# Two layers of graph network and expert mixture: the first expert pages on bytes of their own, and the other pages' transposes moved from three pairs ahead of their products to five

## The chip, the cores and the metric

The kernel runs on one core of one Trainium2 chip. The metric is the device time of one execution in microseconds; it is given as the median of a few runs. The five engines of the core are TensorE (PE, matrix products and transposes; its weight loads are listed as PEld), VectorE (DVE), ScalarE (ACT), GpSimd (POOL) and SyncE (SP). Each engine runs its own instructions in order; semaphores order them against one another. "SPq" and "ACTq" are the DMA queues that SyncE and ScalarE fill; the indirect DMAs of this kernel are issued by GpSimd.

## The reference

The input x has 8,192 tokens (128 graphs of 64 nodes) of 256 numbers, in 32-bit floats. Two layers follow each other, and each has a graph part and an expert part:

```python
x = x + _L0_gnn_ref(_layernorm(x), adj, ...)
x = x + _L0_ffn_ref(_layernorm(x), ...)
x = x + _L1_gnn_ref(_layernorm(x), adj, ...)
x = x + _L1_ffn_ref(_layernorm(x), ...)
```

The change lies in the expert part of layer 0. Each token picks six of 64 experts, and each expert is one 256 x 256 matrix:

```python
def _L0_ffn_ref(x, gate_w, lattice_weights, out_w, out_b, ln_g, ln_b):
    logits = jnp.einsum('bsd,ed->bse', x, gate_w)
    top_logits, indices = jax.lax.top_k(logits, 6)
    scores = jax.nn.softmax(top_logits, axis=-1)
    W_sel = lattice_weights[indices]
    xW = jnp.einsum('bsd,bskde->bske', x, W_sel)
    lattice_out = jnp.einsum('bske,bsk->bse', xW, scores)
    proj = jnp.einsum('bsd,ed->bse', lattice_out, out_w) + out_b
    ...
```

So 8,192 x 6 = 49,152 products of a token's row with its expert's matrix are needed, and their order is free. The graph part of layer 0 (`_L0_gnn_ref`) multiplies each graph's tokens by its adjacency matrix and passes them through a two-layer network of width 1,024; layer 1 is built alike, with eight experts of two matrices each and two experts a token.

## The kernel before

**The stages.** The kernel has four stages, one after the other.

1. Layer 0's graph part and its routing, in 32 blocks of 256 tokens (the long list of functions that ends at line 791). At its end `place` (L745) calls `send` (L310) for each block: 12 indirect DMAs of GpSimd (L314), one for each half of the block and each of the six choices, write every token's normalized row into a table in DRAM (`r0x`), at the place kept for it among its expert's rows. A table row has W = 258 numbers: the 256 values, the number of the answer's row it belongs to, and the weight of the choice. The rows lie in SBUF in the tile `xs` (three buffers).
2. Layer 0's expert pages (lines 800 to 860). The table is read back in pages of 128 rows that all belong to one expert, so that one page needs one matrix.
3. Layer 1's graph part and routing, in 32 blocks again.
4. Layer 1's expert pages, of 256 rows.

**The early pages.** After block 20 the kernel looks (`look`, L151) which of the first twelve experts (EARLY = 12) already have a full page of 128 rows. Such a page gets no more rows, so it can be read while later blocks are still sent. It is the first page of each of these experts: twelve early pages, in six pairs, numbered -6 to -1. All other pages wait for the page table, which VectorE works out after the last block (`page_table`, L338, 810.4 to 829.9 us in the profile). There are 412 of these, in 206 pairs, and a further few behind a branch (L857), for routings that need them.

**One pair of pages** goes through four steps:

- `fetch` (L808): SyncE loads the two pages (129 KB each) from the table into the tile `px`. It has `bufs=22`: 22 pairs may be in SBUF at once. The load of pair j is asked for 12 pairs ahead of its product. `fetch_first` (L456) is the load of an early page, and doesn't wait for rows that are still on their way; `fetch` of the Router (L460) is that of any other. `load_first` and `load` read the page's row numbers into SyncE's registers, four pages at a time.
- `flip` (L822): TensorE transposes the pair, four blocks of 128 x 128, into PSUM (`pt`, L828), and ScalarE copies the result to SBUF (`pxT`, `bufs=5`, L830).
- `apply` (L832): TensorE multiplies (`py`, eight matmuls, L846), with the matrix taken from the tile `lat`, which holds all 64 experts' matrices. For the early pages the expert's number is fixed; for the others TensorE reads it from the page table. VectorE then scales each row by the choice's weight, from PSUM back into the tile `px` (L848). In the same function `fill_end` (L425) has ScalarE's queue write zeros behind one expert's last row (L193), for the pages that are not full.
- `reply` (L319), also called in `apply`: GpSimd writes the page by an indirect DMA to the rows of the answer (`r0y`, L321), one DMA a page. `px` comes free when this has landed.

**What sets the order.** On TensorE, VectorE and ScalarE the order of the instructions is that in which the Python code issues them (`manual_schedule`). `staggered(n, stages, first)` (L466) does the issuing: in step s it calls each stage's function for pair s - lag. With the list at L852 a step s issues the loads of pair s + 12, the product of pair s, and then the transposes of pair s + 2 if that pair is below 4, or of pair s + 3 if it is 4 or above. Between pairs 3 and 4 two transposes follow one another. On SyncE and GpSimd a scheduler sets the order, by what is ready.

**Where tiles lie.** A tile pool (`tc.tile_pool`) is a stretch of SBUF or PSUM that is given back at the end of its `with` block; the next pool takes the same bytes, and the first use of a new tile waits for the last use of the old tiles that lay there. With `reuse_waits="tile"` these waits go by old tile, not by the whole pool: whoever takes bytes of a tile waits for all uses of that tile. Pools grow from one end of SBUF, those with `side="right"` from the other end. The stage-2 pool `wx0` of the kernel before (px and pxT) is taken as soon as stage 1's pools are given back, and lies on their bytes, among them those of the last blocks' `xs`.

**The expert matrices.** The tile `lat` is as large as all 64 matrices, and parts of it hold other things in stage 1. Seven pieces of four experts are therefore loaded after the last block (L797).

Of the kernel before, what the change touches and what calls it, by code (L numbers as in the profile page):

```python
# [9 lines left out]
F32 = mybir.dt.float32  # L10
# [3 lines left out]
ENG = mybir.EngineType  # L14
MAGIC = 12582912.0
AF = mybir.ActivationFunctionType
ALU = mybir.AluOpType
AX = mybir.AxisListType
PSUM = bass.MemoryType.PSUM
P = 128  # L20
# [445 lines left out]
def staggered(n, stages, first=0):  # L466

    for s in range(first + min(lag for lag, _ in stages), n + max(lag for lag, _ in stages)):
        for lag, f in stages:
            if first <= s - lag < n:  # L470
                f(s - lag)
# [3 lines left out]
def two_layer_gnn_moe_kernel(ctx: ExitStack, tc: tile.TileContext, a: dict, out: bass.AP):  # L475
    nc = tc.nc
    x_in, adjT = a["x"], a["adjT"]
    N, D = x_in.shape
# [3 lines left out]
    KD = D // P  # L482
    T = 2
    C = T * P
    NB = N // C
    E0 = a["L0_ffn_lattice_weights"].shape[0]
# [3 lines left out]
    E1, F1, _ = a["L1_ffn_W2"].shape  # L490
    EARLY = 12
# [9 lines left out]
    ident = const.tile([P, P], F32, name="ident")  # L501
# [57 lines left out]
    r0 = Router(tc, const, small, dram, N, D, E0, K0, T, P, 14 * P, 4, "r0", 3)  # L559
    W = r0.W  # L560
# [3 lines left out]
    lat = lat_pool.__enter__().tile([P, E0, KD, D], F32, name="lat")  # L564
# [18 lines left out]
    with tc.tile_pool(name="c0", bufs=1) as c0, \  # L583
# [28 lines left out]
        late = {}  # L612
# [182 lines left out]
        for i in (0, 5, 2, 3, 1, 6, 4):  # L795
            e = E0 - EB * (i + 1)
            nc.sync.dma_start(out=lat[:, e:e + EB], in_=lat_w[:, e:e + EB])  # L797


    with tc.tile_pool(name="wx0", bufs=3, reuse_waits="tile") as wx, \  # L800
            tc.tile_pool(name="pt1", bufs=4, space=PSUM, reuse_waits="tile") as pt_pool, \
            tc.tile_pool(name="py1", bufs=4, space=PSUM, reuse_waits="tile") as py_pool:
        npair = (r0.pages + 1) // 2
        first = -EARLY // 2
        pairs = {j: dict() for j in range(first, npair)}
        regs = {}

        def fetch(j):  # L808
            Q = pairs[j]
            Q["px"] = px = wx.tile([P, 2, W], F32, name="px", bufs=22)  # L810
            for q in range(2):
                i = 2 * j + q
                if i < 0:
                    if i % 4 == 0:
                        regs["row"] = r0.load_first(i + EARLY, ENG.SP)
                    r0.fetch_first(regs["row"][i % 4], px[:, q:q + 1, :])
                elif i < r0.pages:
                    if i % 4 == 0:
                        regs["row"] = r0.load(0, i, ENG.SP)
                    r0.fetch(i, regs["row"][i % 4], px[:, q:q + 1, :])  # L820

        def flip(j):  # L822
            Q = pairs[j]
            pt = pt_pool.tile([P, KD, C], F32, name="pt")
            n = min(2, r0.pages - 2 * j)
            for q in range(n):
                for k in range(KD):
                    nc.tensor.transpose(pt[:, k, ts(q, P)], Q["px"][:, q, ts(k, P)], ident)  # L828
            Q["xT"] = xT = wx.tile([P, KD, C], F32, name="pxT", bufs=5)
            nc.scalar.copy(xT[:, :, :n * P], pt[:, :, :n * P])  # L830

        def apply(j):  # L832
            Q = pairs[j]
            if 0 <= j < E0:
                r0.fill_end(j)
            if j >= 0 and j % 2 == 0:
                regs["e"] = r0.load(1, 2 * j, ENG.PE)
            py = py_pool.tile([P, 2, D], F32, name="py")
            px, xT = Q["px"], Q["xT"]
            n = min(2, r0.pages - 2 * j)  # L840
            for q in range(n):
                i = 2 * j + q
                for k in range(KD):
                    w = lat[:, i + EARLY, k, :] if i < 0 else \
                        lat[:, ds(regs["e"][i % 4], 1), k, :].rearrange("p o d -> p (o d)")
                    nc.tensor.matmul(py[:, q, :], lhsT=xT[:, k, ts(q, P)], rhs=w, start=(k == 0), stop=(k == KD - 1))  # L846
            for q in range(n):
                nc.vector.tensor_scalar(px[:, q, :D], py[:, q, :], px[:, q, D + 1:D + 2], None, op0=ALU.mult)  # L848
                r0.reply(2 * j + q, px[:, q, :], px[:, q, :D])


        stages = ((-12, fetch), (0, apply),  # L852
                  (-2, lambda j: flip(j) if j < 4 else None), (-3, lambda j: flip(j) if j >= 4 else None))
        likely = (r0.likely_pages - EARLY + 3) // 4 * 2
        staggered(likely, stages, first)
        wait = const.tile([1, 4], F32, name="wait")
        with tc.If(r0.needed(2 * likely)):  # L857
            staggered(npair, stages, likely)

            nc.sync.dma_start(out=wait, in_=r0.answer[0:1, 0:4])  # L860
# [7 lines left out]
    wx = ctx.enter_context(tc.tile_pool(name="wx1", bufs=2, side="right", reuse_waits="tile"))  # L868
# [209 lines left out]
    with tc.tile_pool(name="pt4", bufs=2, space=PSUM, reuse_waits="tile") as pt_pool, \  # L1078
# [4 lines left out]
        regs = {}  # L1083

        likely = r1.likely_pages - FIRST
# [64 lines left out]
        stages = (-2, fetch1), (0, flip1), (1, down), (0, up)  # L1150
# [35 lines left out]
```

## Time and profile before

| What | us |
|---|---|
| Time, median of 3 runs (lowest to highest) | 2091.24 (2089.26 to 2092.26) |
| Profiled execution, first to last instruction | 2457.9 |
| Stage 1 in the profile, about | 0 to 800 |
| Last blocks' routing, page table, last sends | 800 to 845 |
| Layer 0's expert pages | 845 to 1508 |
| Layer 1's graph part | 1509 to 1940 |
| Layer 1's expert pages | 1940 to 2458 |

The profile is one execution under the hardware profiler, which takes longer than the timed ones do; mean granted TensorE clock 0.925. The table below cuts it into stretches. Its columns are the stretch in us and its length, then for each engine the busy time (us) and, in brackets, the number of instructions; then the granted TensorE clock as a share of full speed, the busy share of the DMA engines, and GB/s.

| stretch | length | PE | PEld | DVE | ACT | POOL | PEclk | DMA | GB/s |
|---|---|---|---|---|---|---|---|---|---|
| 800 to 845 | 45 | 10.27 (43) | 8.20 (42) | 27.14 (93) | 2.05 (5) | 25.06 (25) | 0.50 | 0.37 | 114 |
| 845 to 1508 | 663 | 526.06 (2557) | 441.49 (2556) | 178.05 (422) | 117.80 (211) | 410.10 (423) | 0.92 | 0.60 | 178 |
| 1940 to 2458 | 518 | 505.84 (2476) | 445.12 (2474) | 118.92 (368) | 179.56 (414) | 216.90 (141) | 0.99 | 0.68 | 158 |

Read it by row: in the second stretch VectorE and ScalarE are busy for 27% and 18% of the time, GpSimd for 62%, TensorE for 79%; in the third TensorE is busy for 98%. In the first, TensorE has work for 10 of 45 us.

### The profile page before, as it was taken

To read this page: it belongs to the slowest core of one execution; us is meant where nothing else is said; L and a number is where in the kernel's file an instruction comes from. 1 tells how busy PE (TensorE), PEld (TensorE's weight loads), DVE (VectorE), ACT (ScalarE), POOL (GpSimd) and SP (SyncE) were. 2 spreads that over 40 slices of the span, in tenths; PEclk is the share of its full clock that TensorE was granted. 3 is DMA by queue.
4 is the path that set the end of the run, shared out by engine and by line. 5 is a ranking of instruction groups with operands and counts; after the bars stand their busy time and mean duration, and the time that the engine had idled before them with its cause. 6 is when DMAs were issued, how large, how long until landed. Compare 5 with 4: busy or idle time off the path is not lost.

```text
span 2457.9 us, 37031 instructions
## 1 busy us (share of the span) xinstructions
PE 2052.3 (83%) x10564; PEld 1757.6 (72%) x10564; DVE 1190.9 (48%) x3989; ACT 1011.3 (41%) x2037; POOL 1153.4 (47%) x1142
## 2 busy tenths in 40 slices
PE   7887888787875478778777877988898899999998
PEld 6776767676764367666666766877777688888887
DVE  5676767667665522222222223777777522222221
ACT  5666656656654011111111112555555433333332
POOL 0345544554545556666666663233333434444444
PEclk9999889999987689899898998999999899999999
DMA  3223433333325578765555535887675477677775
GB/s 108 89 95 115 128 115 120 127 129 108 111 90 196 162 214 235 213 188 174 171 173 172 158 90 206 279 282 237 228 234 163 111 177 170 156 167 162 161 168 111
DMA packets 284093, 398.96 MB, mean 162 GB/s; under 512 B 56536, under 2 KB 237928, under 8 KB 283888
## 3 DMA queue, kind: packets, MB, share of 16 engines
q1 hardware_dynamic: 204032, 247.67, 34.6%
q0 software_dynamic: 64800, 136.14, 18.7%
q10 hardware_dynamic: 15056, 12.69, 1.6%
q8 instruction: 95, 1.56, 0.3%
q14 instruction: 110, 0.90, 0.1%
HBM read 223.89 MB, written 177.69 MB: 163 GB/s over the span
## 4 chain that ended last, share of the span: by engine, by line
PE 50%; another core or an unknown queue 12%; ACT 8%; DVE 8%; issue 8%; DMA 2%; SPq 2%; POOL 1%; ACTq 0%; DVEq 0%; POOLq 0%
PE py L846 10%; PE ph L1122 9%; PE py L1142 9%; PE ps L913 3%; PE pt L828 3%; PE po L924 3%; PE pz L985 3%; PE pc L996 2%; ACT lat L666 2%; ACT pxT L830 2%; PE ph L663 2%; PE ps L76 1%; SPq L460 1%; ACT xs L715 1%
## 5 line engine op out<-in xcount | busy, mean ns | idle before, releaser
L314 POOL DMA_INDIRECT r0x<-xs,r0row x384 | 388.1, 1011 | 439.8 <-issue 327.9
L846 PE MATMUL py<-lat,pxT 128*128 (+1 forms) x1696 | 448.9, 412 | 124.0 <-ACT pxT L830 109.2
L321 POOL DMA_INDIRECT r0y<-px x424 | 411.2, 970 | 262.8 <-DVE px L848 142.5
L846 PEld LDWEIGHTS py<-lat,pxT 128*128 128x128 f32 x1696 | 333.0, 207 | 182.9 <-ACT pxT L830 122.1
L848 DVE TENSOR_SCALAR px<-py,px 128x256 f32<-128x256 f32 x424 | 178.9, 478 | 487.2 <-remote 167.2
L331 POOL DMA_INDIRECT out_x<-py_s,px x138 | 214.6, 1555 | 294.6 <-DMA out_x<-py_s,px 146.8
L830 ACT COPY pxT<-pt 128x512 f32<-128x512 f32 x212 | 118.5, 588 | 566.1 <-remote 215.5
L696 PE MATMUL ps<-lat 128*128 128x256 f32 x1024 | 276.0, 419 | 26.8 <-issue 26.5
L696 PEld LDWEIGHTS ps<-lat 128*128 128x128 f32 x1024 | 217.6, 215 | 68.8 <-issue 34.8
L1124 ACT ACTIVATE phid<-ph,pw 128x256 f32<-128x256 f32 x276 | 130.6, 473 | 322.7 <-issue 212.1
L1122 PE MATMUL ph<-pxT,pw 128*128 128x256 f32 x1104 | 251.1, 381 | 0.7 <-ACT pxT L1113 0.7
L1142 PE MATMUL py<-fw,phid 128*128 (+1 forms) x1104 | 249.7, 379 | 0.0
L663 PE MATMUL ph<-lat 128*128 128x256 f32 x1024 | 234.4, 388 | 5.8 <-DVE lat L685 5.1
L1122 PEld LDWEIGHTS ph<-pxT,pw 128*128 128x128 f32 x1104 | 210.7, 191 | 29.9 <-ACT pxT L1113 1.1
L314 POOL DMA_INDIRECT r1x<-xs,r1row x128 | 126.1, 985 | 210.7 <-DVE bn_rs L961 114.8
L1142 PEld LDWEIGHTS py<-fw,phid 128*128 128x128 f32 x1104 | 204.5, 190 | 25.0
L663 PEld LDWEIGHTS ph<-lat 128*128 128x128 f32 x1024 | 196.3, 194 | 34.1 <-DVE lat L685 3.9
L828 PE MATMUL pt<-ident,px 128*128 128x128 f32 x848 | 137.5, 285 | 38.2 <-DMA px<-r0x 31.7
L666 ACT ACTIVATE lat<-ph,c_L_gnn_b 128x256 f32<-128x256 f32 x256 | 103.1, 470 | 137.1 <-remote 75.5
L828 PEld LDWEIGHTS pt<-ident,px 128*128 128x128 f32 x848 | 113.1, 149 | 63.9 <-DMA px<-r0x 32.5
L1136 DVE TENSOR_SCALAR p<-p 128x2 f32<-128x2 f32 x69 | 13.0, 188 | 228.6 <-ACT p L1135 228.6
L1145 DVE TENSOR_TENSOR py_s<-py,pb 128x512 f32<-128x512 f32 x69 | 47.8, 692 | 154.4 <-PE py L1142 148.4
(296 smaller groups left out, 2916.6 us busy)
## 6 DMA issues: line engine op xcount, KB each, us to landing
px<-r0x SPq DMA_DIRECT2D x424, 129.0 KB
y<-r0y SPq DMA_DIRECT2D x64, 768.0 KB
pw<-in_L_ffn_W1b SPq DMA_DIRECT2D x69, 514.0 KB
px<-r1x SPq DMA_DIRECT2D x69, 258.0 KB
x<-x SPq DMA_DIRECT2D x64, 256.0 KB
pb<-in_L_ffn_b SPq DMA_DIRECT2D x69, 128.0 KB
r0x<-r0filler ACTq DMA_DIRECT2D x64, 129.0 KB
lat<-in_x SPq DMA_DIRECT2D x32, 256.0 KB
```

Source lines behind the costliest of these rows:

```text
L314: i = self.nc.gpsimd.indirect_dma_start(out=self.table[:, :], out_offset=bass.IndirectOffsetOnAxis(ap=row[:, t, k:k + 1], axis=0), in_=xs[ ...
L321: d = self.nc.gpsimd.indirect_dma_start(out=self.answer[:, :], out_offset=bass.IndirectOffsetOnAxis(ap=x[:, self.D:self.D + 1].bitcast(I32 ...
L331: i, d = f"{self.name}add{i}", self.nc.gpsimd.indirect_dma_start(out=self.total[:, :], out_offset=bass.IndirectOffsetOnAxis(ap=x[:, self.D ...
L663: nc.tensor.matmul(ph[:, c, :], lhsT=w1[:, k, ts(2 * j + c, P)], rhs=B["aggT"][:, k, :], start=(k == 0), stop=(k == KD - 1))
L666: nc.scalar.activation(sq[:, 2 * j + c, :], ph[:, c, :], AF.Square, bias=b1[:, 2 * j + c:2 * j + c + 1], scale=1.0)
L696: nc.tensor.matmul(B["po"][:, t, :], lhsT=B["hT"][:, c, ts(t, P)], rhs=w2[:, c, :], start=False, stop=(t == T - 1 and c == KH - 1))
L828: nc.tensor.transpose(pt[:, k, ts(q, P)], Q["px"][:, q, ts(k, P)], ident)
L830: nc.scalar.copy(xT[:, :, :n * P], pt[:, :, :n * P])
L846: nc.tensor.matmul(py[:, q, :], lhsT=xT[:, k, ts(q, P)], rhs=w, start=(k == 0), stop=(k == KD - 1))
L848: nc.vector.tensor_scalar(px[:, q, :D], py[:, q, :], px[:, q, D + 1:D + 2], None, op0=ALU.mult)
L1122: nc.tensor.matmul(ph, lhsT=w[:, k * F1 + c * P:k * F1 + (c + 1) * P], rhs=Q["xT"][:, k, :], start=(k == 0), stop=(k == KD - 1))
L1142: nc.tensor.matmul(py[:, t, :], lhsT=Q["hid"][:, c, ts(t, P)], rhs=fw2[:, ds(e, 1), c, :].rearrange("p o d -> p (o d)"), start=(c == 0), s ...
```

## The change

It has two parts, both in layer 0's expert pages.

**The early pages get a stage of their own.** The twelve pages go into one tile `early`, in a pool `e0`, and their transposed copies into a second pool `e1` on the right side of SBUF, with four buffers. Both pools, and two PSUM pools, are given back before the ring of the other pages is made. The six pairs run through their own `staggered` call, with the transposes two pairs ahead of the products. The purpose is that the loads of the early pages, and the first copies, should not lie on bytes that the last block's sends still read.

**The other pages' transposes run further ahead.** `pxT` gets 8 buffers for 5, `px` gets 19 for 22 to pay for them, and the transposes of pairs 4 and above are issued five pairs ahead of the products, not three; the pairs 0 to 3 stay at two. The purpose is to have more transposed pairs in hand, so that TensorE's product need not wait for ScalarE's copy. The pairs are now numbered from 0.

```diff
+    with tc.tile_pool(name="e0", bufs=1, reuse_waits="tile") as ex, \
+            tc.tile_pool(name="e1", bufs=4, side="right", reuse_waits="tile") as et, \
+            tc.tile_pool(name="ept", bufs=4, space=PSUM, reuse_waits="tile") as pt_pool, \
+            tc.tile_pool(name="epy", bufs=4, space=PSUM, reuse_waits="tile") as py_pool:
+        early = ex.tile([P, EARLY, W], F32, name="early")
+        xTs = {}
+
+        def fetch_early(e):
+            if e % 4 == 0:
+                late["row"] = r0.load_first(e, ENG.SP)
+            r0.fetch_first(late["row"][e % 4], early[:, e:e + 1, :])
+
+        def flip_early(j):
...
+                    nc.tensor.transpose(pt[:, k, ts(q, P)], early[:, 2 * j + q, ts(k, P)], ident)
+            xTs[j] = xT = et.tile([P, KD, C], F32, name="pxT")
+            nc.scalar.copy(xT, pt)
+
+        def apply_early(j):
...
+            for q in range(2):
+                px = early[:, 2 * j + q, :]
+                nc.vector.tensor_scalar(px[:, :D], py[:, q, :], px[:, D + 1:D + 2], None, op0=ALU.mult)
+                r0.reply(0, px, px[:, :D])
+
+        for e in range(EARLY):
+            fetch_early(e)
+        staggered(EARLY // 2, ((-2, flip_early), (0, apply_early)))
+
...
-        first = -EARLY // 2
-        pairs = {j: dict() for j in range(first, npair)}
+        pairs = [dict() for _ in range(npair)]
...
-            Q["px"] = px = wx.tile([P, 2, W], F32, name="px", bufs=22)
+            Q["px"] = px = wx.tile([P, 2, W], F32, name="px", bufs=19)
             for q in range(2):
                 i = 2 * j + q
-                if i < 0:
-                    if i % 4 == 0:
-                        regs["row"] = r0.load_first(i + EARLY, ENG.SP)
-                    r0.fetch_first(regs["row"][i % 4], px[:, q:q + 1, :])
...
-            Q["xT"] = xT = wx.tile([P, KD, C], F32, name="pxT", bufs=5)
+            Q["xT"] = xT = wx.tile([P, KD, C], F32, name="pxT", bufs=8)
...
         stages = ((-12, fetch), (0, apply),
-                  (-2, lambda j: flip(j) if j < 4 else None), (-3, lambda j: flip(j) if j >= 4 else None))
+                  (-2, lambda j: flip(j) if j < 4 else None), (-5, lambda j: flip(j) if j >= 4 else None))
         likely = (r0.likely_pages - EARLY + 3) // 4 * 2
-        staggered(likely, stages, first)
+        staggered(likely, stages)
```

More of the change, by code (lines that the diff above doesn't have):

```diff
@@ L797, in two_layer_gnn_moe_kernel @@
             nc.sync.dma_start(out=lat[:, e:e + EB], in_=lat_w[:, e:e + EB])
+    with tc.tile_pool(name="e0", bufs=1, reuse_waits="tile") as ex, \
[9 more added lines that the diff above has]
+        def flip_early(j):
+            pt = pt_pool.tile([P, KD, C], F32, name="pt")
+            for q in range(2):
+                for k in range(KD):
+                    nc.tensor.transpose(pt[:, k, ts(q, P)], early[:, 2 * j + q, ts(k, P)], ident)
+            xTs[j] = xT = et.tile([P, KD, C], F32, name="pxT")
+            nc.scalar.copy(xT, pt)
+        def apply_early(j):
+            py = py_pool.tile([P, 2, D], F32, name="py")
+            for q in range(2):
+                for k in range(KD):
+                    nc.tensor.matmul(py[:, q, :], lhsT=xTs[j][:, k, ts(q, P)], rhs=lat[:, 2 * j + q, k, :],
+                                     start=(k == 0), stop=(k == KD - 1))
+            for q in range(2):
+                px = early[:, 2 * j + q, :]
[4 more added lines that the diff above has]
+        staggered(EARLY // 2, ((-2, flip_early), (0, apply_early)))
     with tc.tile_pool(name="wx0", bufs=3, reuse_waits="tile") as wx, \
@@ L809, in fetch @@
             Q = pairs[j]
-            Q["px"] = px = wx.tile([P, 2, W], F32, name="px", bufs=22)
+            Q["px"] = px = wx.tile([P, 2, W], F32, name="px", bufs=19)
             for q in range(2):
                 i = 2 * j + q
-                if i < 0:
-                    if i % 4 == 0:
-                        regs["row"] = r0.load_first(i + EARLY, ENG.SP)
-                    r0.fetch_first(regs["row"][i % 4], px[:, q:q + 1, :])
-                elif i < r0.pages:
-                    if i % 4 == 0:
-                        regs["row"] = r0.load(0, i, ENG.SP)
+                if i % 4 == 0:
+                    regs["row"] = r0.load(0, i, ENG.SP)
+                if i < r0.pages:
                     r0.fetch(i, regs["row"][i % 4], px[:, q:q + 1, :])
@@ L833, in apply @@
             Q = pairs[j]
-            if 0 <= j < E0:
+            if j < E0:
                 r0.fill_end(j)
-            if j >= 0 and j % 2 == 0:
+            if j % 2 == 0:
                 regs["e"] = r0.load(1, 2 * j, ENG.PE)
@@ L841, in apply @@
             for q in range(n):
-                i = 2 * j + q
                 for k in range(KD):
-                    w = lat[:, i + EARLY, k, :] if i < 0 else \
-                        lat[:, ds(regs["e"][i % 4], 1), k, :].rearrange("p o d -> p (o d)")
-                    nc.tensor.matmul(py[:, q, :], lhsT=xT[:, k, ts(q, P)], rhs=w, start=(k == 0), stop=(k == KD - 1))
+                    nc.tensor.matmul(py[:, q, :], lhsT=xT[:, k, ts(q, P)],
+                                     rhs=lat[:, ds(regs["e"][(2 * j + q) % 4], 1), k, :].rearrange("p o d -> p (o d)"),
+                                     start=(k == 0), stop=(k == KD - 1))
             for q in range(n):
```

## The prediction

> **What bounds the kernel now.** I read the page's span and chain first, then the line groups, then the stage that the change touches.
>
> ```profile
> span 2457.9 us, 37031 instructions
> ...
> PE 50%; another core or an unknown queue 12%; ACT 8%; DVE 8%; issue 8%; DMA 2%; SPq 2%; POOL 1%; ACTq 0%; DVEq 0%; POOLq 0%
> ...
> L321 POOL DMA_INDIRECT r0y<-px x424 | 411.2, 970 | 262.8 <-DVE px L848 142.5
> ```
>
> The profiled execution lasts 2457.9 us, the timed runs 2091.24: 367 us are in the profile alone. The chain gives 12%, 295 us, to releases that it can't name. So I must find out which waits of this stage are the profile's own. Two pieces of the timeline (start, length, engine, line) tell. First, undisturbed pairs:
>
> ```profile
> 849.17 1.89 PE L846 MATMUL py<-lat,pxT 128*128 128x256 f32 x8
> 850.08 0.97 POOL L321 DMA_INDIRECT r0y<-px  x1 [0.30 <-issue]
> 850.90 0.60 PE L828 MATMUL pt<-ident,px 128*128 128x128 f32 x4
> 851.33 1.89 PE L846 MATMUL py<-lat,pxT 128*128 128x256 f32 x8
> 851.36 0.97 POOL L321 DMA_INDIRECT r0y<-px  x1 [0.30 <-issue]
> ```
>
> TensorE starts a pair every 851.33 - 849.17 = 2.16 us. GpSimd starts a reply every 1.28 us (0.97 busy and 0.30 between), and a pair has two: 2.55 us. GpSimd is the slower, and 424 replies at 1.275 make 541 us. Second, a disturbed pair:
>
> ```profile
> 1056.49 1.89 PE L846 MATMUL py<-lat,pxT 128*128 x8
> 1058.22 0.60 PE L828 MATMUL pt<-ident,px 128*128 128x128 f32 x4
> 1060.44 0.88 DVE L848 TENSOR_SCALAR px<-py,px 128x256 f32<-128x256 f32 x2 [7.90 <-remote]
> 1062.74 0.58 ACT L830 COPY pxT<-pt 128x512 f32<-128x512 f32 x1 [6.62 <-remote]
> ```
>
> TensorE's work of four pairs is recorded by 1058.8, yet ScalarE and VectorE are released only from 1060.4 on, both by something unnamed. Then TensorE in turn waits for a copy:
>
> ```profile
> ACT pxT L830 <- remote: 215.5, 36, 11.3
> ...
> PE py L846 <- ACT pxT L830: 109.2, 45, 6.1
> ```
>
> I take these late releases as mostly the profile's own: the stage lasts 664 us in the profile (844.83 to the end of the last reply at 1509), 123 more than GpSimd's 541, and the timed run has 367 us to lose somewhere. So **in the timed run GpSimd's replies set the stage**, and only what makes GpSimd idle counts. Its largest single idle time is the passage from the sends to the replies:
>
> ```profile
> 834.00 0.97 POOL L314 DMA_INDIRECT r0x<-xs,r0row  x1 [0.30 <-issue]
> 836.79 0.58 ACT L830 COPY pxT<-pt 128x512 f32<-128x512 f32 x1 [31.22 <-DMA r0x<-xs,r0row]
> 837.61 5.29 SPq L456 DMA_DIRECT2D px<-r0x  x10
> ...
> 839.93 0.69 PE L828 MATMUL pt<-ident,px 128*128 128x128 f32 x2 [0.24 <-DMA px<-r0x]
> ...
> 840.41 3.62 PE L846 MATMUL py<-lat,pxT 128*128 128x256 f32 x8
> ...
> 844.07 0.88 DVE L848 TENSOR_SCALAR px<-py,px 128x256 f32<-128x256 f32 x2 [14.20 <-PE py L846]
> 844.83 0.99 POOL L321 DMA_INDIRECT r0y<-px  x1 [9.86 <-DVE px L848]
> ```
>
> The last send starts at 834.00. Ten of the twelve early loads and the first copy wait until it has landed, since px and pxT lie on bytes of the last block's xs. GpSimd could have gone on at 835.27 and does at 844.83: 9.6 us lost.
>
> **What the Trainium skill says.** "DMA: Bandwidth & Descriptors", section "Anatomy of one DMA — SWDGE (gpsimd) path": a GpSimd DMA has some 2 us of fixed cost, most of it the receipt of the write, before its semaphore rises. The trace agrees: the send of 834.00 releases ScalarE 2.79 us after its start. "Perfetto Trace Analysis", section "Tensor Engine Instruction (MATMUL, LD_WEIGHTS)": the recorded end of a matmul is an estimate. That fits releases that come after it, and warns against trusting PE's records in the disturbed stretches; it doesn't prove whose they are. "TensorE: Matmul & The Clock Gate", section "What's actually happening": after about 3.4 us of idleness TensorE runs at half rate until it has been busy as long. The trace agrees: eight matmuls take 3.62 us at 840.41, after the pause, and 1.89 at 849.17.
>
> **The change part by part.**
>
> *Early pages in a tile of their own.* In the built program the first early load no longer waits for block 31's sends but for those of block 30. The twelve sends of block 31 start from 819.64 to 834.00; block 30's last starts at 818.20 and lands 2.8 us later, at 821.0. All twelve loads are issued by about 827 (5.3 us for ten), and the early xT copies, now in a pool on the right side, wait for no send. TensorE starts cold: three flips, then the first apply by 829 (3.6 us). VectorE is busy with the page table until 829.9, so the first product is ready by 831, in good time; the other five pairs cost TensorE 2.2 us each and are done by 842. GpSimd goes from its last send to the replies without a pause: **-9.6 us**.
>
> *The new wait.* The early tile is given back before the px ring is made, and the ring starts on its bytes. The first px load therefore waits for all twelve early replies to have landed, and every later load is queued behind it on SyncE. Before, the px loads began at 843.93, beside the early replies. Now: twelve replies from 835.27, the last starts at 835.27 + 11 x 1.275 = 849.3, and GpSimd is free at 850.6 with nothing to send. The first load is issued 3.6 us after that last start, as 837.61 follows 834.00: 852.9.
>
> *Transposes five ahead.* TensorE's order is now flips 0, 1, 4, apply 0, flips 2, 5, apply 1, flips 3, 6, apply 2, and from there one flip per apply. Apply 0 stands behind flip 4, which needs the tenth px load. Ten loads took 837.61 to 842.6 between first and last issue, 5.0 us, and landed 1.4 to 1.8 us after issue: 852.9 + 5.0 + 1.6 = 859.5. Half a flip 0.4, eight cold matmuls 3.6, and to GpSimd's start 0.8 (844.03 to 844.83): 864.3. GpSimd's new pause is 864.3 - 850.6 = **+13.7 us**. The doubled flips add 0.5 us to each of the first two distances (2.7 and 2.2 to 3.2 and 2.7, against GpSimd's 2.55), which costs it another **+0.7**; before, the same ramp cost 0.1.
>
> *Eight pxT buffers and 19 px instead of 22.* Equal bytes (3 x 2064 against 3 x 2048 a partition). In the steady part the two further flips put copied pairs in front of TensorE, which already has 0.4 us a pair to spare: zero, hidden behind GpSimd's 2.55. Three px buffers fewer shorten the lead of loads over replies from 22 to 19 pairs; loads are asked for 12 ahead, so 7 remain for replies under way, 18 us against a landing of 2.8: zero too. Instruction counts are equal but for a few.
>
> Sum: -9.6 + 13.7 + 0.7 - 0.1 = **+4.7 us, 2096**.
>
> Bounds of the unknown term, the new pause. Low: the first load issued 2.8 us after the last reply's start (ScalarE's release above) and loads 0.36 us apart (one issue is 0.33): tenth landed at 852.1 + 3.2 + 1.4 = 856.7, first reply at 861.5, pause 10.9, sum +1.9 (2093). High: loads 0.87 us apart, as seven were between 843.9 and 850: tenth landed at 862.5, pause 16.7, sum +7.7 (2099). I take the middle, since those ten loads ran on idle queues as these will.
>
> **The rivals.**
>
> *The deeper transposes pay (faster).* For it: 109 us of TensorE waiting for ACT copies. Two more pairs in hand are 2 x 2.16 = 4.3 us of work, more than the mean wait of 109.2/45 = 2.4. Against: those waits follow the unnamed releases, and GpSimd hides TensorE's slack. If a tenth of GpSimd's 133 us behind VectorE (142.5 - 9.9) is in the timed run too, and all of it is recovered: 2096 - 13 = 2083.
>
> *The shorter ring starves GpSimd (slower still).* SyncE's loads and ScalarE's fills alternate on shared semaphores, so a load held for a buffer holds a fill, and this the copies behind it. Against: the 18 us above. Four missed pairs of 2.55 us would make 2096 + 10 = 2106.
>
> *The pauses cancel (no change).* If the tenth load comes as early as the low bound and the clock is still warm (1.9 for 3.6), the pause is 9.2: 2091.
>
> **How the numbers follow.** Forecast 0.56, of which 0.36 above 0.2% (4.2 us) and 0.20 within; deeper transposes 0.24, faster, since whose the unnamed waits are is my weakest step; starved ring 0.11, slower; cancelling 0.09, within. Faster 0.24, same 0.29, slower 0.47. The range, 2081 to 2103, takes in the bounds 2093 and 2099, the cancelling case, the deeper transposes at their size of 2083 and the near part of the starved ring; some 0.12 lie below it and 0.07 above.
>
> **What would show it.** Right: replies of the early pages directly after the last send, at 1.28 us; then one pause of GpSimd of 11 to 17 us; px loads starting only after the twelfth reply. In the profile the deeper transposes should hide part of the unnamed waits, so PE's 109 us should shrink and the profiled span may fall while the timed one doesn't. Wrong: px loads beside the early replies, no second pause, or a timed gain of more than 5 us, which would mean that TensorE's waits for copies are real in timed runs.

## The result: 2110.73 us against 2090.25, and the profile after

The changed kernel takes 2110.73 us (median of 4 runs, 2108.58 to 2112.17), the kernel before 2090.25 beside it (2087.14 to 2092.26): a ratio of 1.0098, with a 95% interval from 1.0081 to 1.0116, or **+20.4 us** (17 to 24). The prediction had 2096 in a range of 2081 to 2103. The direction was right, the size was not.

To read the numbers below one thing is needed: the runs fall into two groups, in one of which every kernel (the kernel before too) takes some 2450 us, in the other some 2090. The group went with the chip (numbers 0, 5, 7 and 14 against 3, 9 and 13; chip 5 came up in two rounds of runs, with some 2450 us in both), so I call them chips *with late releases* and chips *without*; what puts a chip in one group the runs don't show. The profile of before (2457.9 us) belongs to the first group, its times to the second. Each ratio below is against the kernel before on the same chip.

The changed kernel was profiled on a chip without; no profile of the kernel before on such a chip exists. These are lines of its page: span, chain by engine, replies of the other pages, their products.

```profile
span 2110.4 us, 36825 instructions
...
PE 39%; DMA 2%; DVE 1%; ACT 1%; issue 0%; POOL 0%; ACTq 0%; SPq 0%; POOLq 0%
...
L321 POOL DMA_INDIRECT r0y<-px x412 | 401.7, 975 | 140.6 <-DMA r0y<-px 50.3
L875 PE MATMUL py<-lat,pxT 128*128 x1648 | 396.4, 384 | 6.4 <-issue 2.1
```

The recorded execution now lasts as long as the timed ones, and the chain's 12% of unnamed releases are gone. GpSimd's idle time before the 412 replies is 140.6 us, where before had 262.8 for 424. It can be worked out: 412 times the 0.30 to 0.31 between two replies is 126, and one pause of 15.0 makes up the rest. So GpSimd does set the pace of this stage: in the whole of it, that pause is the only one over 1 us. Here is the passage (timeline of the changed kernel: start, length, engine, line):

```profile
660.58 0.97 POOL L314 DMA_INDIRECT r0x<-xs,r0row  x1 [0.30 <-issue]
661.86 0.99 POOL L321 DMA_INDIRECT r0y<-early  x1 [0.30 <-issue]
...
675.95 0.97 POOL L321 DMA_INDIRECT r0y<-early  x1 [0.31 <-issue]
678.72 13.45 SPq L460 DMA_DIRECT2D px<-r0x  x22
680.99 2.38 PE L860 MATMUL pt<-ident,px 128*128 128x128 f32 x8 [10.92 <-DMA px<-r0x]
...
686.19 1.11 PE L860 MATMUL pt<-ident,px 128*128 128x128 f32 x4 [2.82 <-DMA px<-r0x]
687.37 3.75 PE L875 MATMUL py<-lat,pxT 128*128 x8
...
691.93 0.97 POOL L321 DMA_INDIRECT r0y<-px  x1 [15.00 <-DMA px<-r0x]
```

The early replies follow the last send with no pause; the twelfth starts at 675.95; only then, at 678.72, is the first px load issued; eight transposes can go at 680.99, but the first product waits for the third group of transposes (flip 4) at 686.19, and runs cold in 3.75 us. All of this is as the prediction said. What it didn't say is at the other end of the stage:

```profile
1176.16 8.80 PE L875 MATMUL py<-lat,pxT 128*128 x40
...
1185.00 0.88 DVE L879 TENSOR_SCALAR px<-py,px 128x256 f32<-128x256 f32 x2 [0.85 <-PE py L875]
1185.09 1.86 SPq L927 DMA_DIRECT2D y<-r0y  x2
...
1189.94 2.79 PE L944 MATMUL ps<-ident,y 128*128 128x128 f32 x12 [4.98 <-DMA y<-r0y]
...
1203.18 4.63 PE L944 MATMUL ps<-ident,y 128*128 128x128 f32 x24 [4.61 <-DMA y<-r0y]
...
1218.11 1.10 POOL L321 DMA_INDIRECT r0y<-px  x1 [0.30 <-issue]
```

TensorE's last product ends at 1184.96 (40 matmuls, 8.80 us in all, from 1176.16), layer 1's first load of answers (y, L927) goes out at 1185.09, and its transposes start at 1189.94, while GpSimd goes on sending replies until 1219.21, **34.3 us longer**. Layer 1 doesn't wait for them. The kernel says so in `load3` (L898 before):

```python
if b < READY:
    tc.declare_no_dep(d.ins, group="r0last", reason="in the first pages, or waited for above")
```

READY is 5: the first five blocks of layer 1 need rows only of pages that have long been sent. What the first y load does wait for is in the waits of SyncE's queue (who waited for whom: us in all, times, longest):

```profile
SPq L460 <- DMA r0y<-px: 200.7, 152, 4.8
...
SPq L927 <- PEq L888: 8.5, 1, 8.5
```

The second line says that SyncE's first y load waits 8.5 us for TensorE to come to the branch behind the pages (L888), and TensorE comes there when its last products are issued. The first line says that the px loads wait 200.7 us in all for replies to land and give buffers back: the ring holds TensorE to GpSimd's pace. From 1250 us to the end TensorE is the busy engine (834 of 860 us). So the time moves with the moment at which *TensorE* is through with its pages, not with GpSimd's last reply, and this moment depends on how far TensorE may run ahead of GpSimd: as far as the px ring reaches.

### The profile page after: what moved, and what is told of

Read it like the earlier page. It is cut to its first block, busy times and chain, and to the rows that moved or that the text cites. A ratio compares the mean times of both kernels' runs of the same rounds, so it can differ in the third digit from the quotient of the medians.

```text
span 2110.4 us, 36825 instructions
## 1 busy us (share of the span) xinstructions
PE 1949.9 (92%) x10564; PEld 1683.6 (80%) x10564; DVE 1192.5 (57%) x3989; ACT 1019.2 (48%) x2037; POOL 1167.6 (55%) x1142
## 5 line engine op out<-in xcount | busy, mean ns | idle before, releaser
L314 POOL DMA_INDIRECT r0x<-xs,r0row x384 | 395.8, 1031 | 258.6 <-issue 171.1
L321 POOL DMA_INDIRECT r0y<-px x412 | 401.7, 975 | 140.6 <-DMA r0y<-px 50.3
L875 PE MATMUL py<-lat,pxT 128*128 x1648 | 396.4, 384 | 6.4 <-issue 2.1
L875 PEld LDWEIGHTS py<-lat,pxT 128*128 128x128 f32 x1648 | 299.4, 191 | 48.7 <-DVE px L879 8.7
L696 PE MATMUL ps<-lat 128*128 128x256 f32 x1024 | 237.5, 380 | 0.0
L696 PEld LDWEIGHTS ps<-lat 128*128 128x128 f32 x1024 | 193.1, 191 | 24.6
L314 POOL DMA_INDIRECT r1x<-xs,r1row x128 | 130.4, 1019 | 80.3 <-issue 24.1
L860 PE MATMUL pt<-ident,px 128*128 128x128 f32 x824 | 132.0, 279 | 35.6 <-DMA px<-r0x 24.9
L860 PEld LDWEIGHTS pt<-ident,px 128*128 128x128 f32 x824 | 100.9, 142 | 71.0 <-issue 20.9
L687 ACT ACTIVATE lat<-lat,c_L_gnn_rms_weight 128x256 f32<-128x256 f32 x256 | 105.6, 495 | 37.8 <-DVE lat L685 37.4
```

The costliest lines, as they stand in the source:

```text
L314: i = self.nc.gpsimd.indirect_dma_start(out=self.table[:, :], out_offset=bass.IndirectOffsetOnAxis(ap=row[:, t, k:k + 1], axis=0), in_=xs[ ...
L321: d = self.nc.gpsimd.indirect_dma_start(out=self.answer[:, :], out_offset=bass.IndirectOffsetOnAxis(ap=x[:, self.D:self.D + 1].bitcast(I32 ...
L696: nc.tensor.matmul(B["po"][:, t, :], lhsT=B["hT"][:, c, ts(t, P)], rhs=w2[:, c, :], start=False, stop=(t == T - 1 and c == KH - 1))
L875: nc.tensor.matmul(py[:, q, :], lhsT=xT[:, k, ts(q, P)], rhs=lat[:, ds(regs["e"][(2 * j + q) % 4], 1), k, :].rearrange("p o d -> p (o d)") ...
```

## The experiments

**Theory A (the lead).** GpSimd paces the stage, and TensorE ends ahead of it by what the ring allows. Fewer px buffers mean that the last loads wait for later replies; each pair that the transposes run further ahead leaves one more product to do after the last load. Both move layer 1's start. **Theory B:** only GpSimd's pauses count, as in the prediction. **Theory C:** deeper transposes help TensorE. Two further ones, D and E, are put in the expectations of e7 and e8.

### Each part by itself, on chips with late releases: e1 to e4

e1 is the kernel before, unchanged. e2 is the second part alone:

```diff
-            Q["px"] = px = wx.tile([P, 2, W], F32, name="px", bufs=22)
+            Q["px"] = px = wx.tile([P, 2, W], F32, name="px", bufs=19)
-            Q["xT"] = xT = wx.tile([P, KD, C], F32, name="pxT", bufs=5)
+            Q["xT"] = xT = wx.tile([P, KD, C], F32, name="pxT", bufs=8)
-                  (-2, lambda j: flip(j) if j < 4 else None), (-3, lambda j: flip(j) if j >= 4 else None))
+                  (-2, lambda j: flip(j) if j < 4 else None), (-5, lambda j: flip(j) if j >= 4 else None))
```

e3 is the changed kernel with these three numbers as before (22, 5, -3), e4 the kernel before with `bufs=19` for px alone.

> The kernel before, unchanged, for a second profile of it. Its recorded execution took 2457.9 us against 2091 timed, that of the changed kernel 2110.4 against 2110.7. Theory A (the lead): GpSimd sets the pace of the expert pages at 1.28 us a reply, but TensorE runs ahead of it by as much as the px ring allows, and the time is set by when TensorE is through with its pages, because layer 1's graph part, whose first five blocks need none of the last pages, is TensorE's from there on. In an undisturbed profile the pause of GpSimd before the early pages is 9.6 us, and TensorE's last product ends some 45 us before the last reply (34.3 us in the changed kernel, plus 3 px buffers x 2.55 us, plus 2 pairs x 1.76 us). Theory B (the pause alone): the lead is the same in both kernels, some 34 us, and the pause before the early pages is near zero in an undisturbed run, so that the changed kernel's 15.0 us are all new. Time 2090 in either.

> The kernel before with the second part of the change alone: transposes five pairs ahead, 8 pxT buffers, 19 px. Theory A (TensorE's lead over GpSimd counts at the end of the pages): 3 px buffers fewer x 2 replies x 1.278 us = 7.7 us of lead lost, and two more products (1.76 us each) left to do after the last transposes = 3.5 us; together +11.2 us, 2101.5. Theory B (only pauses of GpSimd count, and the early pages' pause makes the whole loss): 2090 to 2091. Theory C (deeper transposes help TensorE): below 2086.

> The changed kernel with its second part undone: 22 px, 5 pxT, transposes three pairs ahead; the early pages keep their own tile. The first px load still waits for the twelve early replies, but the first product no longer stands behind the transposes of the fifth pair, so GpSimd's pause is some 10.6 us for 15.0 (in the changed kernel the first copy ends 682.89 us, eight cold matmuls 3.6, half a microsecond to GpSimd). Theory A: 10.6 - 9.6 = +1.0, and about +1 for slow first pairs: 2092. Theory B (the early stage makes the loss of 20 us): 2105 to 2110.

> The kernel before with 19 px buffers for 22 and nothing else changed. Theory A (lead): +7.7 us, 2098. Theory B (loads have 7 pairs to spare, 18 us, and GpSimd sets the time): 2090 to 2091.

Measured, against 2460.95 us for the kernel before on this chip: e1 2459.91 (0.9997, 0.9981 to 1.0013), **e2 2456.98 (0.9983, 0.9968 to 0.9998)**, e3 2467.94 (1.0027, 1.0011 to 1.0044), e4 2462.53 (1.0002, 0.9985 to 1.0018). None of the expectations fits: e1 isn't at 2090, and the deeper transposes gain 4.2 us (0.5 to 7.9). So the 2458 us of the first profile were not the profiler's doing, as the part on the profile before has it; this kind of chip takes as long when timed. Why e2 gains is in the waits. First e1, then e2:

```profile
ACT pxT L830 <- remote: 179.7, 29, 11.3
...
PE py L846 <- ACT pxT L830: 84.6, 38, 6.1
```

```profile
ACT pxT L830 <- remote: 225.9, 31, 11.6
...
PE py L846 <- ACT pxT L830: 2.0, 2, 1.4
```

ScalarE's copy is released late in both (by the program it can only wait for TensorE; the profile names no releaser), but with five pairs in hand TensorE no longer waits for the copies: 84.6 us become 2.0. The ring alone doesn't do that: e4 has 84.2. GpSimd's idle time between its last send and its last reply, beyond 0.30 a reply, falls with it, from 136 to 120 us. This is theory C, true on this kind of chip. TensorE ends only 21.0 us (e1) and 9.5 us (e2) ahead of the last reply there, and it isn't the ring that holds it. These are waits of SyncE's queue in e1:

```profile
SPq L896 <- PEq L857: 57.1, 1, 57.1
...
SPq L460 <- DMA r0y<-px: 12.2, 10, 3.5
```

The px loads wait for replies 12.2 us in all, and SyncE stands 57.1 us at the branch before TensorE comes. So a shorter ring made no difference that e4 resolves. e3 lost 6.6 us (2.7 to 10.8): at the passage GpSimd has three pauses (3.40, 1.94 and 10.95 us), some 6 us more than the one of 9.82 in e1. None of this says anything on the 20.4 us, measured on the other kind.

### The second part, its ring, and its opposite: e5, e6, e13

e5 is the kernel of e2 again, e13 that of e4, and e6 goes the other way: `bufs=24` for px and `bufs=4` for pxT, which take 2,080 bytes a partition more in all (2 x 2064 - 2048).

> The second part of the change alone (transposes five pairs ahead, 8 pxT, 19 px) once more, since the chip of the first comparison ran every kernel, the kernel before too, at some 2460 us, with long late releases behind TensorE, where the change itself was measured at 2111 against 2090. On a chip that runs the kernel before at 2090: theory A (TensorE's lead over GpSimd at the end of the pages counts) +11.2 us: 3 px buffers x 2.55, and two products x 1.76 more after the last transposes. Theory B (only GpSimd's pauses count): 0 to +1. Theory C (deeper transposes help): below -4. On a chip like the first: -4, as there.

> The kernel before with 24 px buffers for 22 and 4 pxT for 5 (they fit in its bytes). On a chip that runs the kernel before at 2090: theory A: two more pairs of lead, 2 x 2.55 = -5.1 us; in the profile the last product ends some 50 us before the last reply, and GpSimd pauses 9.6 us before the early pages. Theory B: no change, lead some 34 us as in the changed kernel, and a short pause before the early pages. On a chip like the first: no change.

> The kernel before with 19 px for 22, for a chip that runs the kernel before at 2090. Theory A: +6.6 to +7.7 us (ratio 1.0032 to 1.0037): the ring's share of the second part's +11.5 us; the other 4 are the depth. Rival (all is depth): 0.

These ran on chips without late releases. e5: 2102.63 against 2092.54, ratio 1.0055 (1.0035 to 1.0075), **+11.5 us**. e6: 2084.88, 0.9966 (0.9954 to 0.9977), **-7.1 us**. e13: 2097.10 against 2090.56, 1.0035 (1.0025 to 1.0045), **+7.3 us**. Theory A said +11.2, -5.1 and +6.6 to +7.7. B's 0 to +1 and C's gain are out. Of e6's 7.1 some 2.3 aren't the ring's: its pause at the passage is 7.2 us; there four early loads, not two, went out ahead of the last sends. Two further runs of the kernel of e13, e9 and e11, fell on chips with late releases and show no difference there, as e4: 1.0000 (0.9980 to 1.0021) and 0.9994 (0.9970 to 1.0018).

> The kernel before with 19 px for 22 and nothing else, on a chip that runs it at 2090: it splits the +11.5 us of the second part into ring and depth. Theory A: three buffers x 2.2 to 2.55 us = +6.6 to +7.7 (ratio 1.0032 to 1.0037), and the rest, 3.5 to 5, is the depth: two more products left after the last transposes. Rival (the ring isn't what costs, all is the depth): 0.

> The kernel before with 19 px for 22 once more, for a chip that runs the kernel before at 2090; with the late releases it made no difference (1.0000). Theory A: +6.6 to +7.7 us (ratio 1.0032 to 1.0037), the ring's share of the second part's +11.5; in the profile the last px load is issued some 7 us nearer to the last reply than in e6 and e7. Rival (all is depth): 0.

The profile of e5 is the nearest to what the kernel before does at its passage on such a chip:

```profile
658.38 0.97 POOL L314 DMA_INDIRECT r0x<-xs,r0row  x1 [0.30 <-issue]
661.15 0.59 ACT L830 COPY pxT<-pt 128x512 f32<-128x512 f32 x1 [33.77 <-DMA r0x<-xs,r0row]
661.25 5.75 SPq L456 DMA_DIRECT2D px<-r0x  x10
...
668.77 0.99 POOL L321 DMA_INDIRECT r0y<-px  x1 [9.43 <-DVE px L848]
```

GpSimd's pause before the early pages is 9.43 us (9.46 in e13), or 9.1 beyond the usual 0.30, for the 9.6 of the prediction. And TensorE's wait for the copies, which the prediction read as 109 us and then as mostly not there, is 15.1 us in e13 (waits of e13, three pairs ahead):

```profile
PE py L846 <- ACT pxT L830: 15.1, 13, 2.0
```

So there was little for deeper transposes to gain. What they cost shows at the end of the stage. SyncE's last px loads and layer 1's first y load (timeline of SyncE's queue: start, length, line, count), first e13, then e5:

```profile
1130.92 31.72 SPq L460 DMA_DIRECT2D px<-r0x  x26
1171.28 0.81 SPq L896 DMA_DIRECT2D y<-r0y  x2
```

```profile
1129.88 35.36 SPq L460 DMA_DIRECT2D px<-r0x  x28
1176.30 0.82 SPq L896 DMA_DIRECT2D y<-r0y  x2
```

From the end of the last px load to the y load it is 8.6 us in e13 (1130.92 + 31.72 = 1162.64, to 1171.28) and 11.1 in e5. The table has the same for all profiles of chips without late releases. Times are us; the last column is the span from the y load on.

| kernel | px, pairs ahead | pause at the passage | last px load to last reply's end | last px load to y load | y load | span | from y load to the end |
|---|---|---|---|---|---|---|---|
| after | 19, 5 | 15.0 | 46.7 | 12.6 | 1185.09 | 2110.4 | 925.3 |
| e5 | 19, 5 | 9.4 | 44.4 | 11.1 | 1176.30 | 2100.9 | 924.6 |
| e8 | 19, 5 | 3.9 | 45.5 | 11.8 | 1170.76 | 2097.1 | 926.3 |
| e13 | 19, 3 | 9.5 | 46.2 | 8.6 | 1171.28 | 2092.5 | 921.2 |
| e7 | 22, 3 | 10.3 | 57.1 | 8.9 | 1166.12 | 2090.0 | 923.9 |
| e6 | 24, 3 | 7.2 | 61.4 | 9.3 | 1159.63 | 2083.5 | 923.9 |
| e14 | 25, 2 | none | 66.3 | 8.4 | 1153.11 | 2080.2 | 927.1 |

The last column stays within 921 to 927 us while the y load moves by 32 us: the span follows the y load. The time from the last *reply's* end to the end of the span runs from 869 (e14) to 893 (e8), so it isn't the last reply that starts layer 1; in all seven the first y load waits for TensorE at the branch (4.7 to 8.5 us). The fourth column grows with the ring: 45.7 us with 19 (mean of four), 66.3 with 25, of which 5.0 are a pause of GpSimd just before the last reply: (61.3 - 45.7) / 6 = 2.6 us a buffer, two replies. e7 and e6 have such a last pause too, of 3.65 us; without it they have 53.5 with 22 and 57.8 with 24. The fifth is 11.8 at five pairs ahead and 8.9 at three (means): 2.9 us for two products, a little under the two times 1.76 that I expected. Each profile is one execution, and the last send already starts between 657.15 (e13) and 660.58 us (after), so up to 3.4 us of a y load come from ahead of the passage.

How the lead is used also shows in the sixth block, the first whose loads must wait for the last reply. In the four kernels with 19 buffers they wait for no reply; with 22, 24 and 25 they wait 9.7, 12.6 and 16.2 us. Of e14:

```profile
SPq L927 <- DMA r0y<-px: 16.2, 1, 16.2
```

So the lead can be used up to what five blocks give to do. What these waits cost isn't resolved: e14's last column is the highest, by 0.8 to 5.9 us.

### The first part and its new wait: e7, e8

e7 is the kernel of e3 again. e8 is the changed kernel with the early pages in six tiles, so that the first px load waits for two early replies instead of twelve:

```diff
-        early = ex.tile([P, EARLY, W], F32, name="early")
+        early = [ex.tile([P, 2, W], F32, name="early", bufs=EARLY // 2) for _ in range(EARLY // 2)]
...
-                px = early[:, 2 * j + q, :]
+                px = early[j][:, q, :]
```

> The first part of the change alone (early pages in a tile of their own; 22 px, 5 pxT, three pairs ahead) on a chip that runs the kernel before at 2090. Theory A (the time moves with the moment at which TensorE is through with its pages: 9.6 us of pause saved at the last send, a new pause for the twelve replies, ring as before): the first product no longer stands behind the tenth load, so the new pause is some 10.6 us for 15.0: +1 to +3, so a ratio of 1.0005 to 1.0015. Theory D (a stage of its own for the early pages costs something else, which makes the 7 us that the new pause and the shorter lead leave over): +7 or more. On a chip with the late releases: +6, as there.

> The changed kernel with one edit: the twelve early pages lie in six tiles of two pages, where the waits go by tile, so the first px load waits for the first two early replies to land, not for twelve. Theory A: GpSimd's 15.0 us of pause between the twelfth early reply and the first other one go almost wholly, since the loads can start some 10 us before the twelfth reply: 15 less than the changed kernel, so 20.4 - 15 = +5.4 over the kernel before, ratio 1.0026. Theory E (the pause is hidden by something later, the lead is all): +18 to +20 as the changed kernel.

Measured: e7 2095.91 against 2091.51, 1.0020 (1.0010 to 1.0031), **+4.2 us**; its pause is 10.3 us. e8 2098.85, 1.0037 (1.0023 to 1.0051), **+7.7 us**, 12.7 less than the change. The timeline of e8 shows the pause shrink to 3.9:

```profile
673.28 0.97 POOL L321 DMA_INDIRECT r0y<-early  x1 [0.30 <-issue]
678.16 0.97 POOL L321 DMA_INDIRECT r0y<-px  x1 [3.91 <-DMA px<-r0x]
```

11.1 us of pause taken away gave 12.7 us, where each of the two times is known to 3 or 4 us: within that a pause of GpSimd is worth its length, because every later reply, and with it every later load, moves. Theory E is out. e7 is somewhat dearer than the +1 to +3 of theory A; the interval, 2.1 to 6.5, reaches down to that and leaves out D's +7. Two short pauses at 712.60 and 730.12 us (0.85 and 1.24) make some 1.5 us of it.

### A version from the theory: e14 (and e10, e12)

Early pages in six tiles as in e8, and, against the changed kernel:

```diff
-            Q["px"] = px = wx.tile([P, 2, W], F32, name="px", bufs=19)
+            Q["px"] = px = wx.tile([P, 2, W], F32, name="px", bufs=25)
-            Q["xT"] = xT = wx.tile([P, KD, C], F32, name="pxT", bufs=8)
+            Q["xT"] = xT = wx.tile([P, KD, C], F32, name="pxT", bufs=3)
-                  (-2, lambda j: flip(j) if j < 4 else None), (-5, lambda j: flip(j) if j >= 4 else None))
+                  (-2, lambda j: flip(j) if j < 4 else None), (-2, lambda j: flip(j) if j >= 4 else None))
```

> A version from the theory: early pages in six tiles of their own, as in e8, 25 px and 3 pxT, and all transposes two pairs ahead. Theory A: the pause before the first replies saved (9.4 us), a new one of some 2.5 us, three px more x 2.2 to 2.55 us and one product less after the last transposes (1.8): -6.9 - 6.6 - 1.8 = -15, 2076, ratio 0.993. If TensorE has to wait for copies at two pairs ahead (theory C): no gain, or slower than before.

> Early pages in six tiles of their own, 25 px, 3 pxT, all transposes two pairs ahead, once more, for a chip that runs the kernel before at 2090; with the late releases it was slower (1.0047), where TensorE needs transposed pairs in hand. Theory A: -15 us, 2076, ratio 0.993. Theory C (transposes in hand are needed here too): 2090 or more.

> Early pages in six tiles of their own, 25 px, 3 pxT, all transposes two pairs ahead, for a chip that runs the kernel before at 2090. Theory A: -15 us, 2076, ratio 0.993. Theory C (transposes in hand are needed here too): 2090 or more.

e14 ran on a chip without late releases: 2078.44 against 2090.56, **0.9938 (0.9922 to 0.9953), -13.0 us**, where A said -15. Its timeline has no pause between the early and the other replies (a later one, of 2.2 us, stands at 723.07):

```profile
674.32 0.97 POOL L321 DMA_INDIRECT r0y<-early  x1 [0.30 <-DMA px<-r0x]
675.60 0.97 POOL L321 DMA_INDIRECT r0y<-px  x1 [0.31 <-issue]
```

e10 and e12, on chips with late releases, are slower than before: 1.0047 (1.0018 to 1.0075) and 1.0061 (1.0038 to 1.0084). There transposed pairs in hand are needed, as e2 showed, so this version beats both kernels on one kind of chip only.

### Taking the lead's use away: e15 to e18

With `READY = 1` for 5, only one block of layer 1 may start before the last reply. e15 and e17 are the kernel before with it, e16 and e18 that of e2.

> The kernel before with READY = 1 for 5: only layer 1's first block may start before the last reply has landed, so TensorE's lead over GpSimd is worth one block at most. Theory A: the time is now set by the last reply: 1209.7 (last reply's end in e5) + 2 + 925 (TensorE's part after its pages) - 16 for what was done ahead = 2120, +30, ratio 1.014. Rival (the lead isn't used): no change.

> The same with the second part of the change (five pairs ahead, 8 pxT, 19 px) and READY = 1. Theory A: the last reply comes at the same time in both, so the +11.5 us that this part costs with READY = 5 shrink to 0 to 3: about the time of e15. Rival (the second part delays something else, GpSimd or the loads): still +11 over e15.

> The kernel before with READY = 1 for 5, for a chip that runs the kernel before at 2090 (with the late releases, TensorE has little lead and it cost 0.3%). Theory A: the time is set by the last reply: 2120, +30, ratio 1.014. Rival (the lead isn't used): no change.

> The same with the second part of the change and READY = 1, for a chip that runs the kernel before at 2090. Theory A: within 3 us of e17, where the second part alone costs 11.5 us with READY = 5. Rival (the second part delays GpSimd or the loads themselves): 11 us over e17.

All four fell on chips with late releases, where the lead is short: e15 1.0033 (1.0009 to 1.0056), e17 1.0028 (1.0011 to 1.0045), e16 1.0008 (0.9975 to 1.0042), e18 1.0017 (0.9986 to 1.0048). READY costs some 5 to 8 us (the medians differ by 5.4 in both pairs, the ratios say 7 to 8). Beside each other, the second part doesn't cost but gains: e16 is 9.5 us below e15 (2444.52 against 2453.98) and e18 9.8 below e17 (2445.58 against 2455.39), which is theory C on this kind of chip once more. They don't tell A from its rival on the chips where the 20.4 us were measured; this direct test stays open. What stands for A is the table, the wait at the branch, the sixth block's waits, and that A's sizes lie within the intervals of e5, e6, e13 and e14.

## Why the prediction was wrong, point by point

- **GpSimd paces the stage:** right. Replies every 1.28 us, no pause but one in the changed kernel's whole stage.
- **"367 us are in the profile alone":** wrong in its reason. They belong to the kind of chip, not to the profile; e1 takes 2460 timed. The conclusion, that the timed runs of 2091 don't have those late releases, held all the same.
- **Early replies straight after the last send, -9.6:** right: the pause is 9.1 beyond the usual 0.30 in e5, and there is none in the changed kernel.
- **The new wait, +13.7:** right in mechanism and close in size: 15.0, or 14.7 beyond the usual 0.30. The piece that stands behind flip 4 is 15.0 - 10.3 (e7) = 4.7.
- **The ramp, +0.7 - 0.1:** hardly seen: outside the pause at the passage and beyond 0.30 a reply, GpSimd idles 2.4 us (after) against 2.1 (e5) and 2.4 (e13): +0.3 at most.
- **"Only what makes GpSimd idle counts", and from it zero for five pairs ahead and for three px buffers fewer:** this is the step that failed. The working was sound as to GpSimd, for it never starved in the steady part: the rival of the starved ring didn't happen. But the loads' 7 spare pairs were not the question. TensorE runs ahead of GpSimd until the ring stops it, and layer 1 starts when TensorE is done. The zero for the ring measures +7.3 (e13, 5.2 to 9.4). The zero for the depth measures +4.2 (e5 less e13), which isn't clear of the two intervals by itself; the 2.9 us more from the last px load to the first y load stand for it.
- **Deeper transposes pay:** not on the chips of the forecast (15.1 us of waits in e13, and e5 is slower than e13), but on the other kind, -4.2 us (e2).

The measured terms: first part alone +4.2, ring +7.3, depth +4.2, and flip 4 ahead of the first product, which needs both parts, +4.7: together 20.4, against 20.4 measured. The three taken from times are known to 2 to 5 us each, so the close fit is partly chance: the first part and flip 4 make 8.9 us by the times, and 5.6 by GpSimd's pauses alone (15.0 for 9.4).

## What to carry to other kernels

The engine that paces a stage isn't always the one whose end starts the next stage: look which instruction of the next stage comes first, what it waits for, and how far its engine may run ahead. Where that is so, each buffer of the ring was worth one step of the pacing engine at the end (here two replies, 2.6 us), even though the ring never ran dry, as long as the next stage has work that doesn't need the last results; and each step of lookahead left one more step of work after the last load. When a profile lasts much longer than the timed runs, find out first whether both come from the same chip, before explaining its waits away or building on them.

## What was not expected of the hardware

The same program takes 2090 us on some chips and 2450 on others; of the chips seen here none lay between. On the slower, mean granted clock 0.92 to 0.93 against 0.97, ScalarE and VectorE wait up to 12 us for releases that the profile doesn't name while TensorE's recorded work is over, and GpSimd's idle time in the expert pages, beyond 0.30 a reply, is 111 to 140 us where the others have 6 to 17. What is late there the runs don't show. A change can win on the one kind and lose on the other: e2 and e5 are one kernel (-4.2 and +11.5 us), and so are e12 and e14.
